# Neighbourhood attention: groups of 112 keys taken as two column halves of 56, side by side in the TensorE array

## The chip, the cores and the metric

The kernel runs on one core of a Trainium2 chip. The metric is the time of one execution on the device in microseconds; the median of several runs counts. The core has TensorE (PE, matmuls; its weight loads are listed apart as PEld), VectorE (DVE), ScalarE (ACT), GpSimd (POOL) and SyncE (SP, which here only issues DMAs). Each engine takes its own instructions in order and waits on semaphores for the others. Matmuls write to PSUM[...]; VectorE and ScalarE read it.

## The reference

The program is two layers of a network on an image x of shape (2, 256, 56, 56): windowed attention, a mixture of experts, a convolution block, and a second mixture of experts. Only the attention is touched. It has 8 heads of 32 channels; each pixel attends to the 7x7 pixels around it:

```python
q = _proj(x, wq, bq).reshape(Bt, NUM_HEADS, hd, Hh, Ww)
k = _proj(x, wk, bk).reshape(Bt, NUM_HEADS, hd, Hh, Ww)
v = _proj(x, wv, bv).reshape(Bt, NUM_HEADS, hd, Hh, Ww)
kw = _windows(k, WINDOW)
vw = _windows(v, WINDOW)
attn = jnp.einsum('bhdxy,bhdxyw->bhxyw', q, kw) * scale
attn = jax.nn.softmax(attn, axis=-1)
out = jnp.einsum('bhxyw,bhdxyw->bhdxy', attn, vw).reshape(Bt, C, Hh, Ww)
```

`_windows` pads by three and stacks the 49 shifted copies; padded positions have key and value zero and count in the softmax.

## The kernel before

The image is cut into 14 strips of 8 rows (7 for each of the two pictures), and a strip into four groups of 14 columns, so that a group has 8x14 = 112 keys. The attention is taken from the side of the keys: the queries that can see any key of a group lie in the 14x20 pixels around it (14 rows by 17 columns in the outer groups of a strip, 11 rows in the strips at the picture's upper and lower edge), that is 280, 238, 220 or 187 queries.

A loop over the strips runs eight steps in each: four groups (`tx`) by two halves of the channels (`c`, four heads each). One step consists of

- `scores`: four f32 matmuls (L1495), one for each head, with 32 rows of keys (32x112) as weights and the queries as moving operand, in four row tiles of the array; then four bf16 matmuls (L1504) that add a mask of -1e30 where a query doesn't see a key, as a product of two small tables (`hot_w`, `far_w`). They go to two PSUM tiles `sc` of two heads (two banks) each, of a pool with two buffers. ScalarE then takes the exponential of each tile (`ex`, L1514).
- `attend`, always of the step before: for each pair of heads `j` two matmuls (L1524) with the values of 112 keys as weights (64 columns: 32 of value and 32 ones, which give the softmax's denominator) into one PSUM bank `av` of a pool with two buffers, and one VectorE addition of that bank into `acc` (L1534), the sums of all queries of the picture in SBUF.
- a piece of `project` for the strip two ahead (layer norm, the transposed `xc`, keys, queries, values), and a piece of what is under way: `leave` (division by the denominators, output projection) and the routing of the first experts.

The program's order is the order on each engine: `scores` of this step, `attend` of the step before, the piece of `project`, the piece of `leave` and routing. All semaphores are set by the framework, from the tiles that an instruction reads and writes. In `project`, queries are evacuated from PSUM by VectorE (L1459), keys by ScalarE (L1455), values by two VectorE additions (L1477), each on a half of one PSUM bank. `blocks` is the view that turns rows of 56 columns into groups of 14; it is used here and in later stages wherever the order of tokens (by groups) meets the order of pixels. Its input `x_tok` is put into token order on the host.

Of the kernel before, what the change touches and what calls it, by code (L numbers as in the profile page):

```python
# [11 lines left out]
F32 = mybir.dt.float32  # L12
# [9 lines left out]
P = 128  # L22
# [20 lines left out]
TT = NQ  # L43
NTT = NT // TT
# [589 lines left out]
def metaformer(ctx: ExitStack, tc: tile.TileContext, a: dict, out: bass.AP, flag):  # L634
# [610 lines left out]
    def blocks(ap):  # L1245

        return ap.rearrange("p h (t w) -> p t h w", w=TW)
# [105 lines left out]
    with ExitStack() as st:  # L1353
# [38 lines left out]
        for n in "vo":  # L1392
            bias[n] = (aw if n == "o" else sw).tile([TT, C], F32, tag=f"b{n}", name=f"b{n}")
            nc.sync.dma_start(bias[n], a[f"L0_conv_b{n}_row"].partition_broadcast(TT))
        hot_w = sw.tile([P, TT], BF16, tag="hot_w", name="hot_w")
        far_w = sw.tile([P, KR, KW], BF16, tag="far_w", name="far_w")
        parts = tp.tile([P, NTT, PAIRS, TT], F32, tag="taken", name="parts", bufs=1)
        far_f = parts[:, 0].rearrange("p j n -> p (j n)")[:, :NK]
        hot_f = parts[:, 1, 0, :]
# [18 lines left out]
        for i in range(3):  # L1418
            t = sw.tile([TT, NTT, PAIRS, 4, HD], F32, tag=f"vals{i}", name=f"vals{i}")
            nc.gpsimd.memset(t[:, :, :, 1:3, :], 1.0)  # L1420
            vals.append(t)
        keys = {}
        norm0, settle0, tiles0, _, gates0, wgt0, counted0, _ = routing(0, aw, tp, ps)

        def project(g):
# [5 lines left out]
            xc = sp.tile([P, KC, NT], F32, tag="xc", name="xc")  # L1431
            for k in range(KC):
# [7 lines left out]
                nc.scalar.copy(xc[:, k, :], px[:, :NT])  # L1440
            yield
            keys[g] = sp.tile([P, KC, NT], F32, tag="keys", name="keys", bufs=3)
            for n in "kq":
                for o in range(KC):
                    pj = ps.tile([P, 512], F32, tag="aux", name="pj")
                    for k in range(KC):
# [3 lines left out]
                            xc[:, k, :],  # L1450
# [7 lines left out]
                    else:  # L1458
                        nc.vector.tensor_scalar_add(  # L1459
                            blocks(q_im[:, o, s * SR : (s + 1) * SR, :]),  # L1460
                            pj[:, :NT].rearrange("p (t h w) -> p t h w", h=SR, w=TW),
                            bias[n][:, o : o + 1],
                        )
                yield
            for t in range(0, NTT, 2):
                pj = ps.tile([TT, 2, C], F32, tag="aux", name="pv")
                for i in range(2):
                    for k in range(KC):
                        nc.tensor.matmul(
                            pj[:, i, :],  # L1470
                            xc[:, k, (t + i) * TT : (t + i + 1) * TT],
# [13 lines left out]
        def scores(g, tx, c):  # L1485

            s = g % NS
            r0, r1 = max(0, s * SR - APAD), min(H, (s + 1) * SR + APAD)
            c0, c1 = max(0, tx * TW - APAD), min(W, (tx + 1) * TW + APAD)
            y0, x0 = APAD - s * SR, APAD - tx * TW  # L1490
            nq = (r1 - r0) * (c1 - c0)
            sc = [sps.tile([TT, 2, 512], F32, tag="sc", name="sc") for _ in range(2)]
            for h in range(4):
                p = slice(HD * h, HD * (h + 1))
                nc.tensor.matmul(  # L1495
                    sc[h // 2][:, h % 2, :nq],
                    keys[g][p, c, tx * TT : (tx + 1) * TT],
                    q_im[p, c, r0:r1, c0:c1],
                    start=True,
                    stop=False,  # L1500
                )
            for h in range(4):
                p = slice(HD * h, HD * (h + 1))
                nc.tensor.matmul(  # L1504
                    sc[h // 2][:, h % 2, :nq],
                    hot_w[p, :],
                    far_w[p, y0 + r0 : y0 + r1, x0 + c0 : x0 + c1],
                    start=False,
                    stop=True,
                )  # L1510
            ex = []
            for j in range(2):
                e = sp.tile([TT, 2, NK], F32, tag="ex", name="ex", bufs=4)
                nc.scalar.activation(e[:, :, :nq], sc[j][:, :, :nq], AF.Exp, scale=HD**-0.5)  # L1514
                ex.append(e)
            return g, tx, c, (r0, r1, c0, c1), ex

        def attend(g, tx, c, window, ex):
            r0, r1, c0, c1 = window
            nq = (r1 - r0) * (c1 - c0)  # L1520
            for j in range(2):
                av = sps.tile([P, 512], F32, tag="av", name="av")
                for i in range(2):
                    nc.tensor.matmul(  # L1524
                        av[VW * i : VW * (i + 1), :nq],
                        vals[g % 3][:, tx, 2 * c + j, 2 * i : 2 * i + 2, :].rearrange(
                            "p a d -> p (a d)"
                        ),
                        ex[j][:, i, :nq],
                        start=True,  # L1530
                        stop=True,
                    )
                d = acc[:, 2 * c + j, r0:r1, c0:c1]
                added = nc.vector.tensor_tensor(  # L1534
                    d, av[:, :nq].rearrange("p (h w) -> p h w", w=c1 - c0), d, ALU.add
                )
            pace[:] = [added.ins]

        def leave(g):
# [36 lines left out]
            for i in range(2):  # L1576
                at = slice(3 * HD * i, 3 * HD * i + HD)
                for j in range(2):
                    to = HD * (2 * j + i)
                    for k in range(KC):  # L1580
                        nc.vector.tensor_tensor(
                            oc[to : to + HD, k, :].rearrange("p (t h w) -> p t h w", h=SR, w=TW),
# [167 lines left out]
    with mid:  # L1750

        with ExitStack() as st:
# [20 lines left out]
            def combine(i):  # L1773
# [13 lines left out]
                for k in range(KC):  # L1787
                    nc.scalar.copy(
                        blocks(inner(*STRIPS[i])[:, :, k]),
                        pu[:, k].rearrange("p (t h w) -> p t h w", h=SR, w=TW),  # L1790
# [296 lines left out]
        with ExitStack() as both:  # L2087
# [17 lines left out]
            def residual(i):  # L2105
# [7 lines left out]
                for at in range(1 + paced):  # L2113
                    for o in range(KC):
# [5 lines left out]
                        if at or not paced:  # L2120
                            nc.scalar.activation(
                                nr[:, o].rearrange("p (t h w) -> p t h w", h=SR, w=TW),
# [158 lines left out]
    with ExitStack() as st:  # L2281
        tp = st.enter_context(tc.tile_pool(name="last_t", bufs=2, reuse_waits="tile"))
        ps = st.enter_context(tc.tile_pool(name="last_ps", bufs=2, space=PSUM, reuse_waits="tile"))
        for i, (b, s) in enumerate(STRIPS):
# [4 lines left out]
            for k in range(KC):  # L2289
                nc.scalar.copy(  # L2290
                    blocks(o[:, k].rearrange("p (h w) -> p h w", w=W)),
                    pu[:, k].rearrange("p (t h w) -> p t h w", h=SR, w=TW),
# [25 lines left out]
def _window_parts():  # L2318


    ky, kx = np.divmod(np.arange(TT), TW)
    rows, cols = np.arange(SR)[:, None], np.arange(TW)[:, None]
    hot = np.concatenate([ky == rows, kx == cols]) * MASKED
    qy, qx = np.divmod(np.arange(NK), KW)
    far = np.concatenate([abs(qy - APAD - rows) > APAD, abs(qx - APAD - cols) > APAD])
# [4 lines left out]
def _laid_out(inputs):  # L2330
    i = {n: np.asarray(v) for n, v in inputs.items()}

    def per_channel(v):
# [5 lines left out]
        i["x"].reshape(B, C, NS, SR, NTT, TW).transpose(0, 2, 3, 5, 4, 1).reshape(-1, TT, NTT, C)  # L2339
# [72 lines left out]
```

## Time and profile before

| | |
|---|---|
| median of three runs | 1844.94 us (1838.95 to 1848.16) |
| profiled execution | 1836.06 us, span of its records 1834.3 us |
| PE, DVE, ACT, POOL busy | 1523.4, 978.8, 701.5, 656.1 us |
| attention loop, first scores to last acc addition | 41.8 to 516 us |
| score matmuls, mask matmuls, attend matmuls | 4 of each in a step, 448 of each |
| acc additions | 224, 0.34 to 0.45 us each |
| exponentials | 224, 0.46 to 0.64 us each |

The page gives for a group of instructions its line, engine, operation and tiles, how many there are, the busy time and mean duration, and the idle time of the engine ahead of it with what ended that. A timeline line gives the start, the duration, the engine, the line, and in brackets the idle time ahead. f32 matmuls are recorded as two instructions each. PEclk is the share of the TensorE clock that was granted.

### The profile page before, as it was taken

The numbers are of one execution on the slowest core, as the hardware profiler recorded it, in microseconds if no ns is written. First come the engines' busy times: TensorE is split into PE (matmuls) and PEld (weight loads), VectorE is DVE, ScalarE is ACT, GpSimd is POOL, SyncE is SP. The second block draws the span as 40 slices with busy tenths as digits, with TensorE's granted clock in tenths as the row PEclk, the third lists the DMA queues.
The fourth block names the chain that finished last, engine by engine and source line by source line (L and its number), as shares of the span: only waits on it lengthen the run. The fifth ranks groups of instructions, "written<-read, shape, count | busy, mean of one in ns | idle before, by whom it ended". The sixth has DMA issues, their size and how long they took to land. (4 is left out here: it accounts for less than half of the span.)

```text
span 1834.3 us, 25840 instructions
## 1 busy us (share of the span) xinstructions
PE 1523.4 (83%) x8612; PEld 1191.8 (65%) x8612; DVE 978.8 (53%) x2690; ACT 701.5 (38%) x1362; POOL 656.1 (36%) x664
## 2 busy tenths in 40 slices
PE   6999998899788858894899799666468799999964
PEld 3555565555466747782788687556457688988953
DVE  4467556476645336855999897675422211111137
ACT  3454433434333324643454443233243333333322
POOL 3012524335343663442244144154553322222210
PEclk9999988999888979996999899755579899999985
DMA  7022324212267757985652000033635568888858
GB/s 241 27 82 83 108 88 122 58 56 83 57 192 232 248 192 265 308 274 161 166 161 61 1 1 1 21 114 99 226 129 186 179 232 273 286 276 294 287 181 311
DMA packets 91886, 291.77 MB, mean 159 GB/s; under 512 B 20487, under 2 KB 35803, under 8 KB 80416
## 3 DMA queue, kind: packets, MB, share of 16 engines
q1 hardware_dynamic: 66736, 231.79, 39.8%
q0 software_dynamic: 21200, 51.82, 8.1%
q10 hardware_dynamic: 3808, 6.42, 1.0%
q8 instruction: 70, 1.15, 0.3%
q14 instruction: 72, 0.59, 0.1%
HBM read 218.51 MB, written 74.20 MB: 160 GB/s over the span
## 5 line engine op out<-in xcount | busy, mean ns | idle before, releaser
L1139 PE MATMUL ph<-ut,w 128*128 128x256 f32 (+1 forms) x1472 | 316.8, 366 | 32.7 <-ACT h L1146 27.5
L1158 PE MATMUL py<-w,h 128*128 128x256 f32 x1288 | 304.1, 385 | 0.0
L1139 PEld LDWEIGHTS ph<-ut,w 128*128 128x128 f32 x1472 | 255.1, 198 | 63.5 <-ACT h L1146 29.0
L1168 DVE TENSOR_TENSOR y<-py,w 128x512 f32<-128x512 f32 (+1 forms) x120 | 76.8, 640 | 409.6 <-PE py L1158 358.2
L888 POOL DMA_INDIRECT xs<-u,pos x224 | 218.1, 974 | 168.6 <-issue 84.4
L1158 PEld LDWEIGHTS py<-w,h 128*128 128x128 f32 x1288 | 247.4, 194 | 34.6 <-DVE y L1168 0.4
L1170 POOL DMA_INDIRECT ys<-y,dest x136 | 136.7, 1005 | 269.9 <-DVE dest L1114 161.0
L1146 ACT ACTIVATE h<-ph,w 128x256 f32<-128x256 f32 (+1 forms) x368 | 162.4, 448 | 115.6 <-PE ph L1139 84.4
L1514 ACT ACTIVATE ex<-sc 112x476 f32<-112x476 f32 (+3 forms) x224 | 117.0, 571 | 207.0 <-PE sc L1504 172.9
L1111 ACT COPY ut<-pt 128x512 f32<-128x512 f32 (+1 forms) x120 | 65.3, 544 | 320.0 <-PE pt L1107 234.2
L1524 PE MATMUL av<-ex,vals 112*64 112x238 f32 (+3 forms) x896 | 125.9, 403 | 16.2 <-DVE acc L1534 15.0
L1534 DVE TENSOR_TENSOR acc<-av,acc 128x238 f32<-128x238 f32 (+3 forms) x224 | 88.1, 408 | 95.4 <-PE av L1524 72.1
L1832 PE MATMUL pc<-lo,wq 128*128 128x448 f32 x336 | 131.5, 393 | 7.3 <-DVE lo L1807 7.2
L1832 PE MATMUL pc<-hi,wq 128*128 128x448 f32 x336 | 131.0, 392 | 3.2 <-DVE x L1856 3.0
L1170 POOL DMA_INDIRECT ys<-y,to x81 | 82.4, 1018 | 128.3 <-DVE dest L1114 74.7
L1975 PE MATMUL pc<-hi,wq 128*128 128x448 f32 (+1 forms) x288 | 102.8, 366 | 18.0 <-ACT hi L1942 9.4
L1229 DVE SCALAR_TENSOR_TENSOR x<-got,wgt,x 112x256 f32<-112x256 f32 x216 | 102.4, 546 | 28.1 <-DMA got<-ys 27.6
L1495 PE MATMUL sc<-q_im,keys 32*112 32x238 f32 (+3 forms) x896 | 95.6, 431 | 11.6 <-ACT ex L1514 7.4
L1975 PE MATMUL pc<-lo,wq 128*128 128x448 f32 (+1 forms) x288 | 101.8, 363 | 0.2 <-DVE lo L1943 0.2
L1524 PEld LDWEIGHTS av<-ex,vals 112*64 112x64 f32 x896 | 57.1, 143 | 66.1 <-issue 26.8
L1107 PE MATMUL pt<-ident,xg 128*128 128x128 f32 x434 | 72.4, 288 | 26.3 <-ACT ut L1111 21.0
L1805 POOL TENSOR_TENSOR v<-pad 128x928 f32<-128x928 f32 (+1 forms) x28 | 56.3, 2023 | 100.3 <-DVE lo L1807 49.1
(273 smaller groups left out, 2467.2 us busy)
## 6 DMA issues: line engine op xcount, KB each, us to landing
w<-in_L_experts SPq DMA_DIRECT2D x64, 1154.0 KB
w<-in_L_experts SPq DMA_DIRECT2D x56, 641.0 KB
xg<-xs SPq DMA_DIRECT2D x97, 260.0 KB
got<-ys SPq DMA_DIRECT2D x28, 896.0 KB
acc<-in_fresh SPq DMA_DIRECT2D x14, 896.0 KB
xt<-in_x_tok SPq DMA_DIRECT2D x14, 448.0 KB
xr<-in_x_tok SPq DMA_DIRECT2D x14, 448.0 KB
rec<-shares SPq DMA_DIRECT2D x28, 224.0 KB
```

The lines of the kernel that those rows point to most:

```text
L888: w = nc.gpsimd.indirect_dma_start(xs[:, :], bass.IndirectOffsetOnAxis(ap=pos[:, j, t0 + t : t0 + t + 1], axis=0), us[t // NTT][:, t % NTT ...
L1139: nc.tensor.matmul(ph[:, :g], w1[:, k, f * P : (f + 1) * P], d["ut"][:, k, :g], start=k == 0, stop=k == KC - 1,)
L1146: nc.scalar.activation(d["h"][:, f, :g], ph[:, :g], AF.Gelu, bias=b1[:, f : f + 1])
L1158: nc.tensor.matmul(py[:, i, :], d["h"][:, f, i * P : (i + 1) * P], w2[:, f, :], start=f == 0, stop=f == NF - 1,)
L1170: o = nc.gpsimd.indirect_dma_start(ys[:, :], bass.IndirectOffsetOnAxis(ap=d["to"][:, i : i + 1], axis=0), y[:, i, :], None, bounds_check=T ...
L1229: nc.vector.scalar_tensor_tensor(xt[:, t, :], y[:, t, j, :], wgt[:, j, n : n + 1], xt[:, t, :], ALU.mult, ALU.add)
L1495: nc.tensor.matmul(sc[h // 2][:, h % 2, :nq], keys[g][p, c, tx * TT : (tx + 1) * TT], q_im[p, c, r0:r1, c0:c1], start=True, stop=False,)
L1514: nc.scalar.activation(e[:, :, :nq], sc[j][:, :, :nq], AF.Exp, scale=HD**-0.5)
L1524: nc.tensor.matmul(av[VW * i : VW * (i + 1), :nq], vals[g % 3][:, tx, 2 * c + j, 2 * i : 2 * i + 2, :].rearrange("p a d -> p (a d)"), ex[j ...
L1534: added = nc.vector.tensor_tensor(d, av[:, :nq].rearrange("p (h w) -> p h w", w=c1 - c0), d, ALU.add)
L1832: nc.tensor.matmul(pc[:, :NT], wq[:, k, c, dx * C + o * P : dx * C + (o + 1) * P], part[:, :, k, dx : dx + W], start=m == 0, stop=m == 2 * ...
L1975: nc.tensor.matmul(pc[:, : 2 * ns * W], wq[:, k, c, dx * C + o * P : dx * C + (o + 1) * P], part[:, : 2 * ns, k, dx : dx + W], start=m == ...
```

## The change

A group of 112 keys becomes two halves of 8 rows by 7 columns, 56 keys each. The queries that see a half lie in 14x13 pixels, 182 (143 in strips of 11 rows); at the picture's side edges the score window is shifted inwards and keeps its 13 columns, and `attend` takes only the 10 columns that see the half. A half takes 64 partitions: the first the partitions 0 to 55, the second 64 to 119.

- `scores`: each head has two matmuls, one for each half, with 56 weight columns, at array columns 0 and 64, and two mask matmuls. `sc` is one tile for the whole loop, four banks, one for each head; the two channel halves `c` share a bank, 256 columns each. It is filled with zeros once, since the exponential now reads all 128 partitions.
- `ex` is taken for two heads at once as before, on 128 partitions and 2x182 elements.
- `attend`: each `j` has four matmuls (two heads by two halves) with 56 rows and 64 columns, and two additions into `acc`, one for each half. `av` is one tile for the whole loop, two banks: one for each half, with both `j` in it, 256 columns each.
- `project`: `xc` holds each half in 64 columns, of which eight stay zero, in two fixed buffers; values are projected with all 128 columns; queries are evacuated by ScalarE.
- Tokens lie by halves; `blocks` works with 7 columns, here and in the later stages, and `x_tok`, `hot` and `far` are laid out to fit.

```diff
+HT = TT // 2
+HW = TW // 2
+HP = P // 2
+WH = HW + WIN - 1
+FAR_W = WH + 2 * APAD
...
-        return ap.rearrange("p h (t w) -> p t h w", w=TW)
+        return ap.rearrange("p h (t w) -> p t h w", w=HW)
...
-            t = sw.tile([TT, NTT, PAIRS, 4, HD], F32, tag=f"vals{i}", name=f"vals{i}")
+            t = sw.tile([P, NTT, PAIRS, 4, HD], F32, tag=f"vals{i}", name=f"vals{i}")
...
+        xcs = []
+        for i in range(2):
+            t = sw.tile([P, KC, 2 * NTT, HP], F32, tag=f"xc{i}", name=f"xc{i}")
+            nc.gpsimd.memset(t[:, :, :, HT:], 0.0)
+            xcs.append(t)
+        sc = sps.tile([P, HEADS // 2, KC, 256], F32, tag="sc", name="sc", bufs=1)
+        av = sps.tile([P, 2, 2, 256], F32, tag="av", name="av", bufs=1)
+        for h in range(HEADS // 2):
+            nc.vector.memset(sc[:, h], 0.0)
...
-                        nc.vector.tensor_scalar_add(
+                        nc.scalar.activation(
                             blocks(q_im[:, o, s * SR : (s + 1) * SR, :]),
-                            pj[:, :NT].rearrange("p (t h w) -> p t h w", h=SR, w=TW),
-                            bias[n][:, o : o + 1],
+                            pj[:, :NT].rearrange("p (t h w) -> p t h w", h=SR, w=HW),
+                            AF.Identity,
+                            bias=bias[n][:, o : o + 1],
                         )
...
-            sc = [sps.tile([TT, 2, 512], F32, tag="sc", name="sc") for _ in range(2)]
+            halves = []
+            for i in range(2):
+                left = (2 * tx + i) * HW
+                c0 = min(max(0, left - APAD), W - WH)
+                halves.append((left, c0, c0 - left + 2 * APAD, slice(HP * i, HP * i + HT)))
             for h in range(4):
                 p = slice(HD * h, HD * (h + 1))
-                nc.tensor.matmul(
-                    sc[h // 2][:, h % 2, :nq],
-                    keys[g][p, c, tx * TT : (tx + 1) * TT],
-                    q_im[p, c, r0:r1, c0:c1],
-                    start=True,
-                    stop=False,
-                )
+                for i, (_, c0, _, at) in enumerate(halves):
+                    nc.tensor.matmul(
+                        sc[at, h, c, :nq],
+                        keys[g][p, c, (2 * tx + i) * HT : (2 * tx + i + 1) * HT],
+                        q_im[p, c, r0:r1, c0 : c0 + WH],
+                        start=True,
+                        stop=False,
+                    )
...
-                e = sp.tile([TT, 2, NK], F32, tag="ex", name="ex", bufs=4)
-                nc.scalar.activation(e[:, :, :nq], sc[j][:, :, :nq], AF.Exp, scale=HD**-0.5)
+                e = sp.tile([P, 2, KR, WH], F32, tag="ex", name="ex", bufs=4)
+                nc.scalar.activation(
+                    e[:, :, : r1 - r0].rearrange("p i h w -> p i (h w)"),
+                    sc[:, 2 * j : 2 * j + 2, c, :nq],
+                    AF.Exp,
+                    scale=HD**-0.5,
+                )
...
+            parts = []
+            for left, c0, _, at in halves:
+                a0, a1 = max(0, left - APAD), min(W, left + HW + APAD)
+                parts.append((a0, a1, slice(a0 - c0, a1 - c0), at, (r1 - r0) * (a1 - a0)))
             for j in range(2):
-                av = sps.tile([P, 512], F32, tag="av", name="av")
                 for i in range(2):
-                    nc.tensor.matmul(
-                        av[VW * i : VW * (i + 1), :nq],
-                        vals[g % 3][:, tx, 2 * c + j, 2 * i : 2 * i + 2, :].rearrange(
-                            "p a d -> p (a d)"
-                        ),
-                        ex[j][:, i, :nq],
-                        start=True,
-                        stop=True,
-                    )
-                d = acc[:, 2 * c + j, r0:r1, c0:c1]
-                added = nc.vector.tensor_tensor(
-                    d, av[:, :nq].rearrange("p (h w) -> p h w", w=c1 - c0), d, ALU.add
-                )
+                    for half, (_, _, cols, at, nq) in enumerate(parts):
+                        nc.tensor.matmul(
+                            av[VW * i : VW * (i + 1), half, j, :nq],
+                            vals[g % 3][at, tx, 2 * c + j, 2 * i : 2 * i + 2, :].rearrange(
+                                "p a d -> p (a d)"
+                            ),
+                            ex[j][at, i, : r1 - r0, cols],
+                            start=True,
+                            stop=True,
+                        )
+                for half, (a0, a1, _, _, nq) in enumerate(parts):
+                    d = acc[:, 2 * c + j, r0:r1, a0:a1]
+                    added = nc.vector.tensor_tensor(
+                        d, av[:, half, j, :nq].rearrange("p (h w) -> p h w", w=a1 - a0), d, ALU.add
+                    )
             pace[:] = [added.ins]
```

## The prediction

> **What bounds the kernel now.** The page comes first. Its chain of waits (part 4) accounts for only a third of the span and names nothing of the attention loop, so it can't be followed back to the change. The place is found from the groups of part 5 and the tiles instead: the score matmuls (tile sc) run from 41.8 to 508.6 us and the acc adds end at 516 us. The loop of 14 strips of 8 steps, 112 steps in all, lasts 474 us. Then busy time by stretch of that loop:
>
> ```profile
> core 0: us, PE busy (x) PEld busy (x) DVE busy (x) ACT busy (x) POOL busy (x), PEclk, DMA share, GB/s
> 42.00:122.00 80.00, 79.97 (x613) 45.38 (x613) 41.75 (x116) 38.95 (x76) 12.73 (x18) 1.00 0.17 55
> 122.00:225.00 103.00, 96.34 (x731) 57.91 (x725) 67.33 (x193) 47.29 (x90) 35.94 (x43) 1.00 0.33 98
> 225.00:351.00 126.00, 114.40 (x766) 70.86 (x764) 71.51 (x208) 45.56 (x92) 46.55 (x54) 0.85 0.31 92
> 351.00:454.00 103.00, 97.43 (x706) 56.73 (x705) 63.94 (x171) 44.82 (x84) 46.33 (x52) 0.98 0.23 67
> 454.00:516.00 62.00, 46.36 (x405) 28.03 (x405) 38.43 (x119) 20.04 (x40) 25.42 (x28) 0.85 0.26 73
> ```
>
> PE is busy for 434.5 of these 474 us (the sum of its column), VectorE for 283, ScalarE for 197. PE sets the pace: whatever lengthens PE's own sequence lengthens the program, and VectorE has room. So the next view is one undisturbed step in order of time:
>
> ```profile
> 149.84 0.68 PE L1495 MATMUL sc<-q_im,keys 32*112 32x238 f32 x8
> 150.34 0.28 PE L1504 MATMUL sc<-far_w,hot_w 32*112 32x238 bf16 x4
> 150.55 1.02 PE L1524 MATMUL av<-ex,vals 112*64 112x238 f32 x8
> 151.22 0.81 DVE L1534 TENSOR_TENSOR acc<-av,acc 128x238 f32<-128x238 f32 x2 [0.52 <-PE av L1524]
> 151.51 1.98 PE L1469 MATMUL pv<-wv,xc 128*112 128x256 f32 x8
> ...
> 153.53 0.76 DVE L1477 TENSOR_TENSOR vals<-pv,bv 112x256 f32<-112x256 f32 x2 [1.50 <-PE pv L1469]
> ```
>
> and the same part of a step with 280 queries:
>
> ```profile
> 436.36 0.75 PE L1495 MATMUL sc<-q_im,keys 32*112 32x280 f32 x8
> 436.94 0.29 PE L1504 MATMUL sc<-far_w,hot_w 32*112 32x280 bf16 x4
> 437.17 1.16 PE L1524 MATMUL av<-ex,vals 112*64 112x280 f32 x8
> 438.26 0.64 PE L1447 MATMUL pj<-xc,wq 128*128 128x448 f32 x1
> ```
>
> From starts to starts, the score phase (sc until av) takes 0.71 us at 238 queries and 0.81 at 280; the attend phase (av until the next group) 0.96 and 1.09. An f32 matmul leaves two records, so x8 is four matmuls. In the score phase all four run beside each other, in attend two and two. The first acc add starts 0.67 us after av; meanwhile PE goes on with the second pair, which has a PSUM tile of its own.
>
> The vals line matters most. PE writes two halves of one bank (i=0, i=1) one after the other, and VectorE adds each half separately. VectorE sat idle for 1.50 us and began the first half only when the matmuls of both were done (151.51 + 1.98 = 153.49). In the trace only the last pv matmul updates a semaphore. So here an engine waits for every access to a bank, also to the half that it doesn't touch.
>
> **What the Trainium skill says.** "PSUM — Partial Sum Buffer", section "PSUM bank collisions raise a hardware error": two engines on one bank and quadrant at once collide, whatever columns they touch, so semaphores have to guard the bank and not the address. The vals wait agrees. "TensorEngine Tiling (Array Packing)", "Key Properties": tiles run in parallel and a change of tiling mode drains the array. The trace agrees on the first: eight records in 0.50 us. The same page, "PSUM Bottleneck": tiling speeds up TensorE and not the evacuation of PSUM. The add rows below agree: they cost by element and by instruction. "TensorE: Matmul & The Clock Gate", "A second HAM failure mode: psum-queue depth-cycling": micro-idles between groups can bring the clock down. The trace has half-clock stretches in this loop (mean clock 0.85 from 225 to 351 us).
>
> **The change, part by part.**
>
> *Score and mask matmuls.* 8 and 8 for 4 and 4 per step, in 32x64 tiles, all eight beside each other, always with 14x13 = 182 queries (143 in strips at the image's edge) for 238 or 280. From 238 to 280 the time from sc to mask grew from 0.50 to 0.58 us, two passes, so 0.95 ns per column and pass; attend grew by 0.13 over four passes, 0.8 ns. I take 0.85. The score phase becomes 0.71 - 2x56x0.85 = 0.62 us: 0.09 or 0.19 less. If the doubled loads show, 0.05 comes back.
>
> *Attend matmuls without waits.* 8 for 4, four beside each other, twice: 0.96 - 4x56x0.85 = 0.77 us, 0.19 or 0.32 less.
>
> *Adds.* Four of at most 182 elements for two of 238 or 280:
>
> ```profile
> L1534 DVE TENSOR_TENSOR acc<-av,acc 128x280 f32<-128x280 f32 x58 | 24.8, 446 | 21.2 <-PE av L1524 14.6 <-remote 3.8 <-PE pj L1447 1.5
> L1534 DVE TENSOR_TENSOR acc<-av,acc 128x238 f32<-128x238 f32 x60 | 23.9, 405 | 30.6 <-PE av L1524 29.1 <-DMA x_mid<-xr 1.1 <-PE sc L1504 0.3
> L1534 DVE TENSOR_TENSOR acc<-av,acc 128x187 f32<-128x187 f32 x24 | 7.8, 351 | 13.4 <-PE av L1524 8.1 <-remote 5.1
> ```
>
> 182 elements cost 0.35 us, so a step costs 1.4 us for 0.81 to 0.89: +0.5 x 112 = 56 us on VectorE. Moving q_im away takes off 28 x 0.67 = 19. VectorE has 320 of 474 us then: no bound by itself.
>
> *The new wait.* Before, av had two buffers and the pairs j=0 and j=1 alternated: an attend waited for adds of the step before. Now av is one tile [P, half, j, 256] of f32: a half's bank holds both j. The matmuls of j=1 follow the adds of j=0 in program order and write the banks that these adds read. By the vals line, PE must wait for both adds. Counted from av's start: adds can begin at 0.67 less two shorter passes (0.10) = 0.57; two adds end at 1.27; 0.05 to release PE (attends that waited for an add here started 0.053 us after its end); then the second half of the attend phase, 0.5 x 0.77 + 0.12 for a refill = 0.50. Attend is 1.82 us for 0.96 or 1.09: +0.86 or +0.73. Below, the wait could cost nothing (if the halves were tracked by columns); above, VectorE's queue is added to it. Behind the waiting matmul stands all of PE's queue: projection, routing, the next scores.
>
> *Net per step*: +0.86 - 0.09 = 0.77 with 238, +0.73 - 0.19 = 0.54 with 280; half of the steps each, 0.65. The 32 steps with 11 rows come to nearly the same, as adds and passes shrink together. 112 x 0.65 = **+73 us**.
>
> *VectorE's queue.* The adds of j=0 stand behind the normalisation (oc, eight of 0.61 us) and residual work, which today's spare av buffer hides. In the strip from 420 to 454 us, replayed by hand with the durations above, PE waits another 0.55, 1.1 and 0.95 us, less 1.59 us that it no longer waits for q_im. Some +1 per strip, up to 3: **+14** (0 to 40).
>
> *What goes away.* Scores wait for exp today (7.4 us on PE, 18.3 on weight loads, not all of it felt); the longer attend covers exp, which shrinks to 128x364 (0.47 us by its rows of 374, 478 ns, and 440, 532 ns): **-10**. PE is idle for 39.5 us of the loop, much of it while ScalarE or POOL finishes a chain of its own; with longer steps some is absorbed: **-12**.
>
> *Clock.* PE idles about 0.45 us more per step, and over 1 us where VectorE is behind. More half-clock windows: **+15** (0 to 45).
>
> *The rest at about nothing.* q_im on ScalarE (28 x 0.63 us, against 27 us saved on exp; ScalarE is 41% busy; uncovered 18). Runs of 7 for 14 in the blocks copies and oc (0 to 7 us on VectorE, 0 to 3 in later stages). Weight loads of 128 for 112 columns in pv hide under 0.22 us passes. Fills of sc, xc and vals at the start lie beside the loads until 41.8 us; uncovered 3. Memory traffic is unchanged.
>
> Sum: 73 + 14 - 10 - 12 + 15 = **+80 us** on the profiled execution's 1836 us, so 1916. The median shown is 1845, 9 us above that execution: **1925**.
>
> **Rivals.** *A, faster:* j=1 isn't held back by the adds of j=0, because the waits go by columns. Then the phases shrink to 0.62 and 0.77: 0.28 or 0.51 less, 0.4 x 112 = 44 us less than 1845, 1801. For it: PE is the bound. Against it: the vals line. It decides where the stall costs less than 0.4 us a step. 7%. *B, about even:* the bank wait exists but most steps cover it, for instance because other waits take the same time today; 1845. Against it: 80 of 80 us busy until 122 us leave nothing to absorb. 5%. *C, much slower:* VectorE's queue and the clock multiply the stall: upper ends 40 and 45 instead of 14 and 15, 1925 + 56 = 1981. For it: the spare buffer that smoothed VectorE's bursts is gone, and the clock already falls to 0.85. 20%. *The forecast:* 68%, 1885 to 1960 on its own.
>
> The range that leaves out A and the extremes of C is 1872 to 1985. Faster by over 0.5% (about what a measurement can tell from no change) 8%, within it 5%, slower 87%.
>
> **What would show it.** The attend group splits in two with an idle of about 0.45 us on PE between, put down to the acc add; step lengths of 2.4 us for 1.67 where no other work lies between; 448 adds near 350 ns; exp no longer waited for; loop end near 595 us. It is wrong if attend runs through in 0.8 us, or if the eight score matmuls take turns.

## The result, and the profile after

The changed kernel takes **1936.97 us** (median of four runs, 1929.5 to 1944.42), the kernel before 1846.55 us beside it: a ratio of 1.0496, with a 95% interval of 1.0439 to 1.0552, so 4.4 to 5.5% slower. The prediction said 1925 us. The profiled execution took 1929.5 us, its records span 1927.7 us: 93 us more than the 1834.3 us of before.

The attention loop, from the first score matmul to the last acc addition, runs from 41.9 to 602.9 us, where it ran from 41.8 to 516.5. That is 561 us for 475, so 86 of the 93 us lie in the loop. The busy time by stretch, as it was shown for the kernel before, with the cuts at the beginnings of strips:

```profile
core 0: us, PE busy (x) PEld busy (x) DVE busy (x) ACT busy (x) POOL busy (x), PEclk, DMA share, GB/s
41.90:132.70 90.80, 82.67 (x1084) 41.17 (x1083) 47.34 (x160) 36.36 (x81) 9.44 (x16) 0.98 0.14 43
132.70:255.20 122.50, 116.20 (x1213) 62.50 (x1213) 70.86 (x233) 46.71 (x99) 38.02 (x41) 0.83 0.27 81
255.20:391.90 136.70, 120.26 (x1245) 67.70 (x1244) 76.12 (x254) 44.27 (x98) 47.37 (x56) 0.81 0.29 87
391.90:515.20 123.30, 109.91 (x1186) 58.69 (x1185) 65.66 (x213) 42.46 (x90) 44.39 (x50) 0.86 0.19 55
515.20:603.00 87.80, 69.46 (x747) 37.24 (x746) 47.16 (x166) 16.32 (x40) 27.20 (x32) 0.61 0.19 52
```

Two things are to be seen. The first row holds strips 0 to 2 (24 steps): PE is idle for 8 of 90.8 us, where it was busy without a gap before, and the three strips take 90.8 us for 79.9, at nearly full clock in both kernels. Below it the clock falls to 0.81 to 0.86, in the last row to 0.61; before, the stretches had 1.00, 1.00, 0.85, 0.98 and 0.85. In this trace the clock is granted either whole or at one half, so each row's time at half clock is 2 x (1 - PEclk) x its length. Over the loop the clock records add up to 198 us at half clock after, and 60 before.

The groups of the page for the same operations as before:

```profile
L1568 DVE TENSOR_TENSOR acc<-av,acc 128x182 f32<-128x182 f32 (+3 forms) x448 | 145.3, 324 | 199.9 <-PE av L1557 151.9
L1539 ACT ACTIVATE ex<-sc 128x364 f32<-128x364 f32 (+1 forms) x224 | 89.8, 451 | 239.7 <-PE sc L1529 187.1
L1557 PE MATMUL av<-ex,vals 56*64 56x182 f32 (+3 forms) x1792 | 139.9, 377 | 40.1 <-DVE acc L1568 36.7
L1519 PE MATMUL sc<-q_im,keys 32*56 32x182 f32 (+1 forms) x1792 | 111.6, 375 | 12.9 <-ACT ex L1539 11.7
```

PE stands idle before attend for 40.1 us, 36.7 of them because of an acc addition (15.0 before); that is only a third of a microsecond per step. The timeline of PE and VectorE in strip 1 shows why it is no more:

```profile
67.46 0.56 PE L1519 MATMUL sc<-q_im,keys 32*56 32x182 f32 x16
...
67.82 0.29 PE L1529 MATMUL sc<-far_w,hot_w 32*56 32x182 bf16 x8
68.04 0.47 PE L1557 MATMUL av<-ex,vals 56*64 56x143 f32 x8
...
68.44 0.70 PE L1452 MATMUL px<-ident,xn 112*128 112x112 f32 x5
68.58 0.61 DVE L1568 TENSOR_TENSOR acc<-av,acc 128x143 f32<-128x143 f32 x2 [0.26 <-PE av L1557]
...
69.15 0.51 PE L1519 MATMUL sc<-q_im,keys 32*56 32x182 f32 x2
69.59 0.47 PE L1557 MATMUL av<-ex,vals 56*64 56x143 f32 x8
69.99 0.40 PE L1519 MATMUL sc<-q_im,keys 32*56 32x182 f32 x7
70.03 0.26 PE L1529 MATMUL sc<-far_w,hot_w 32*56 32x182 bf16 x1
70.13 0.61 DVE L1568 TENSOR_TENSOR acc<-av,acc 128x143 f32<-128x143 f32 x2 [0.93 <-PE av L1557]
```

The attend of a step is in two groups, as predicted: the second begins at 69.59, after the two additions have ended at 69.19. But the time between isn't empty. The compiled program has a piece of the projection (px) and the first score matmul of the next step there, and the rest of those scores after the second group. The section on the kernel before says that the program's order is the order on each engine. For TensorE the compiled program departs from it where there is a wait: in the kernel before, 109 of 112 steps have their attend matmuls in one piece, after, nearly every step has them in two, with other matmuls that the framework's scheduler put between. Here the prediction's picture doesn't fit.

### The profile page after: what moved, and what is told of

The parts are those of the page before. It is cut to its first block, busy times and chain, and to the rows that moved or that the text cites. A ratio compares the mean times of both kernels' runs of the same rounds, so it can differ in the third digit from the quotient of the medians.

```text
span 1927.7 us, 30415 instructions
## 1 busy us (share of the span) xinstructions
PE 1580.1 (82%) x10852; PEld 1196.6 (62%) x10852; DVE 997.9 (52%) x2890; ACT 693.4 (36%) x1390; POOL 656.2 (34%) x666
## 5 line engine op out<-in xcount | busy, mean ns | idle before, releaser
L1568 DVE TENSOR_TENSOR acc<-av,acc 128x182 f32<-128x182 f32 (+3 forms) x448 | 145.3, 324 | 199.9 <-PE av L1557 151.9
L1539 ACT ACTIVATE ex<-sc 128x364 f32<-128x364 f32 (+1 forms) x224 | 89.8, 451 | 239.7 <-PE sc L1529 187.1
L1557 PE MATMUL av<-ex,vals 56*64 56x182 f32 (+3 forms) x1792 | 139.9, 377 | 40.1 <-DVE acc L1568 36.7
L1557 PEld LDWEIGHTS av<-ex,vals 56*64 56x64 f32 x1792 | 53.7, 153 | 126.9 <-DVE acc L1568 76.7
L1519 PE MATMUL sc<-q_im,keys 32*56 32x182 f32 (+1 forms) x1792 | 111.6, 375 | 12.9 <-ACT ex L1539 11.7
L1112 PEld LDWEIGHTS pt<-ident,xg 128*128 128x128 f32 x434 | 56.5, 148 | 57.2 <-issue 29.1
```

Of the source, the lines that this page charges most:

```text
L1112: nc.tensor.transpose(pt[:, k, i * P : (i + 1) * P], d["xg"][:, i, k * P : (k + 1) * P], ident)
L1519: nc.tensor.matmul(sc[at, h, c, :nq], keys[g][p, c, (2 * tx + i) * HT : (2 * tx + i + 1) * HT], q_im[p, c, r0:r1, c0 : c0 + WH], start=Tru ...
L1557: nc.tensor.matmul(av[VW * i : VW * (i + 1), half, j, :nq], vals[g % 3][at, tx, 2 * c + j, 2 * i : 2 * i + 2, :].rearrange("p a d -> p (a ...
L1568: added = nc.vector.tensor_tensor(d, av[:, half, j, :nq].rearrange("p (h w) -> p h w", w=a1 - a0), d, ALU.add)
```

## The experiments

The first theory is the prediction's: with both `j` in one bank (512 f32 values of each partition, the size of the kernel's PSUM tiles of `[P, 512]`), the attend of j=1 waits for the additions of j=0, and the idle time brings the clock down. The main rival is that smaller matmuls and their many changes of tile shape cost the time, wait or no wait.

Chips differ: the kernel before took 1856.29 us on the chip of the first four experiments, 1747.83 on that of the next four, and 1850.46 on that of the last four. So ratios are to the kernel before on the same chip, and loops are compared only where the kernel before took about the same. For each kernel, worked out from the records of its profiled execution: the loop's length, its time at half clock, PE's idle time in it, and how often the tile shape (rows and columns rounded up to 32, 64 or 128) changes from one matmul record to the next. The expectations quoted below took the time at half clock a little too low: 56 us where the records give 60, 194 for 198, 267 for 271.

| kernel | median us | ratio (interval) | loop us | half clock us | PE idle us | changes |
|---|---|---|---|---|---|---|
| before | 1846.55 | 1 | 475 | 60 | 40 | 322 |
| changed | 1936.97 | 1.0496 (1.0439 to 1.0552) | 561 | 198 | 62 | 562 |
| e1_adds_last | 1886.74 | 1.0194 (1.0149 to 1.0238) | 509 | 163 | 84 | 325 |
| e2_merged_adds | 1867.3 | 1.0066 (1.0033 to 1.0099) | 490 | 139 | 79 | 326 |
| e3_before_one_av | 1928.06 | 1.0385 (1.0341 to 1.0428) | 554 | 170 | 24 | 547 |
| e4_q_on_vector | 1953.64 | 1.054 (1.0504 to 1.0575) | 574 | 221 | 68 | 573 |
| e5_before_q_scalar | 1743.13 | 0.9974 (0.9959 to 0.999) | 456 | 47 | 30 | 319 |
| e6_in_order | 1899.35 | 1.0845 (1.0792 to 1.0898) | 611 | 271 | 134 | 310 |
| e7_in_order_filled | 1893.28 | 1.0833 (1.0807 to 1.0859) | 604 | 260 | 129 | 310 |
| e8_merged_q_vector | 1791.36 | 1.0246 (1.0225 to 1.0268) | 498 | 156 | 76 | 336 |
| e9_filled_matmuls | 2016.29 | 1.089 (1.0807 to 1.0972) | 642 | 268 | 110 | 310 |
| e10_in_order_again | 2033.17 | 1.0979 (1.0913 to 1.1045) | 651 | 329 | 161 | 310 |
| e11_merged_again | 1876.44 | 1.0134 (1.0078 to 1.019) | 489 | 140 | 79 | 326 |
| e12_merged_q_vector_again | 1900.23 | 1.0263 (1.0204 to 1.0322) | 519 | 175 | 86 | 336 |

The last three columns show one thing that the first theory doesn't cover. In the eleven kernels with 310 to 340 changes of shape, the time at half clock is 1.5 to 2.5 times PE's idle time. In the three whose groups are cut up (the changed kernel, e3 and e4, with 547 to 573 changes) it is 3.2 to 7.1 times. So idle time as the profile counts it is not all that goes with a low clock here; what else counts isn't shown.

### e1: all attend matmuls ahead of the additions

The changed kernel, with the matmuls of both `j` first and the four additions after them. The work is the same, only the wait inside a step goes.

```diff
             for j in range(2):
                 for i in range(2):
                     for half, (_, _, cols, at, nq) in enumerate(parts):
                         nc.tensor.matmul(
...
+            for j in range(2):
                 for half, (a0, a1, _, _, nq) in enumerate(parts):
```

> The changed kernel, with the matmuls of both j ahead of the four adds in attend, so that the wait inside a step goes and only the wait for the adds of the step before is left. Wait theory (the time lies in the wait of the second attend group for the adds of the first, and in what follows from it: split groups and a falling clock): 1790 to 1850 us, half-clock stretches in the loop well under the 194 us of the changed kernel, near the 56 us of the kernel before. Small-tile theory (the time lies in twice as many small matmuls, weight loads and changes of tile shape): above 1910 us, half-clock time little changed.

Moving the additions takes 52 us off the loop and the changes of tile shape back to 325. The wait inside the step, with the cutting up of groups that goes with it, is the largest part of the loss. It isn't all: the time is above what the first theory expected, and the half-clock time stays at 163 us. The next step's attend still finds both banks taken by the additions just issued: PE's idle time put down to additions is 38.8 us, where the changed kernel has 36.7. PE's idle time in all rises to 84 us; most of the rise (14 us) stands before instructions for which the profile names no wait.

### e2: e1 with one addition for both j of a half

```diff
-            for j in range(2):
-                for half, (a0, a1, _, _, nq) in enumerate(parts):
-                    d = acc[:, 2 * c + j, r0:r1, a0:a1]
-                    added = nc.vector.tensor_tensor(
-                        d, av[:, half, j, :nq].rearrange("p (h w) -> p h w", w=a1 - a0), d, ALU.add
-                    )
+            for half, (a0, a1, _, _, nq) in enumerate(parts):
+                d = acc[:, 2 * c : 2 * c + 2, r0:r1, a0:a1]
+                added = nc.vector.tensor_tensor(
+                    d, av[:, half, :, :nq].rearrange("p j (h w) -> p j h w", w=a1 - a0), d, ALU.add
+                )
```

> As e1_adds_last, with the two j of a half added by one instruction of 2x182 elements: two adds in a step for four. Wait theory: 5 to 20 us below e1_adds_last, since the next step's attend waits for two adds of about 0.54 us instead of four of 0.35. Small-tile theory: as e1_adds_last, above 1910 us.

Another 19 us, down to 0.3 to 1.0% above the kernel before. Its timeline shows the phases without the wait inside the step, and the wait that is left:

```profile
70.80 1.02 DVE L1568 TENSOR_TENSOR acc<-av,acc 128x280 f32<-128x280 f32 x2 [0.96 <-PE av L1557]
...
71.88 0.85 PE L1557 MATMUL av<-ex,vals 56*64 56x182 f32 x16 [0.56 <-DVE acc L1568]
72.66 0.99 PE L1452 MATMUL px<-ident,xn 112*128 112x112 f32 x8
...
73.57 0.56 PE L1519 MATMUL sc<-q_im,keys 32*56 32x182 f32 x16
73.93 0.29 PE L1529 MATMUL sc<-far_w,hot_w 32*56 32x182 bf16 x8
74.14 0.85 PE L1557 MATMUL av<-ex,vals 56*64 56x182 f32 x16
```

The score phase takes 0.57 us (73.57 to 74.14; in the kernel before 0.71 or 0.81) and attend 0.78 us (71.88 to 72.66; before 0.96 or 1.09). So the halves do make PE's own work shorter, by 0.32 us with 238 queries and 0.55 with 280. The single `av` buffer then takes it back: at 71.88 PE has waited 0.56 us for the addition of the step before. At 74.14 it waits for nothing, since a piece of the projection (px) lay between.

### e3: the kernel before with one av buffer

One `av` buffer for two, nothing else: no smaller matmuls, only the wait.

```diff
-                av = sps.tile([P, 512], F32, tag="av", name="av")
+                av = sps.tile([P, 512], F32, tag="av", name="av", bufs=1)
```

> The kernel before, with one buffer for av instead of two: the wait of the second attend group for the add of the first, without the small tiles. Wait theory: 1880 to 1960 us, and more than 120 us at half clock in the loop. Small-tile theory: within 1% of the kernel before, because other work fills the gap.

The kernel before becomes 3.4 to 4.3% slower with its large matmuls. This decides against small matmuls as such, as the origin of a loss of this size. Its timeline shows the same pattern as the changed kernel:

```profile
145.85 0.62 PE L1524 MATMUL av<-ex,vals 112*64 112x238 f32 x4
146.41 0.51 PE L1495 MATMUL sc<-q_im,keys 32*112 32x280 f32 x3
146.43 0.32 PE L1504 MATMUL sc<-far_w,hot_w 32*112 32x280 bf16 x1
146.52 0.41 DVE L1534 TENSOR_TENSOR acc<-av,acc 128x238 f32<-128x238 f32 x1 [1.04 <-PE av L1524]
...
147.47 1.20 PE L1524 MATMUL av<-ex,vals 112*64 112x280 f32 x4
```

Half an attend, then parts of the next scores, then the addition, then the next half (at half clock here). PE's idle time even falls, from 40 to 24 us, while the loop grows by 80. A wait that the scheduler fills shows as more busy time, not as idle time: a group cut in two takes longer than in one piece (two times 0.62 us here for one of 1.02), the scores are cut up as well, and the tile shape changes 547 times for 322. The first two strips show this price alone, since they have no half clock and hardly any idle time. First the kernel before:

```profile
41.80:65.10 23.30, 23.27 (x195) 13.69 (x195) 10.83 (x30) 11.31 (x24) 6.73 (x8) 1.00 0.28 89
65.10:91.30 26.20, 26.20 (x204) 14.31 (x203) 11.24 (x31) 12.85 (x24) 1.43 (x3) 1.00 0.06 19
```

and then e3:

```profile
42.40:69.20 26.80, 26.63 (x193) 13.16 (x192) 11.13 (x30) 11.27 (x24) 6.46 (x8) 1.00 0.22 73
69.20:99.00 29.80, 29.62 (x201) 13.41 (x200) 11.39 (x31) 12.72 (x24) 1.42 (x3) 1.00 0.05 16
```

That is 7.1 us in 16 steps, 0.44 us per step. How it divides between longer groups and changes of shape wasn't tried. Over the whole loop e3 is also 170 us at half clock for 60, with less idle time than before.

### e4, e5, e8, e11 and e12: who takes q_im

e4 is the changed kernel with q_im back on VectorE; e5 is the kernel before with q_im on ScalarE; e8 and e12 are e2 with q_im on VectorE, and e11 is e2 again beside e12.

```diff
-                        nc.scalar.activation(
+                        nc.vector.tensor_scalar_add(
                             blocks(q_im[:, o, s * SR : (s + 1) * SR, :]),
                             pj[:, :NT].rearrange("p (t h w) -> p t h w", h=SR, w=HW),
-                            AF.Identity,
-                            bias=bias[n][:, o : o + 1],
+                            bias[n][:, o : o + 1],
                         )
```

> The changed kernel with the queries evacuated by VectorE again (28 instructions of about 0.67 us). Wait theory: 0 to 15 us above the changed kernel, as the adds stand behind them in VectorE's queue. A theory in which ScalarE's new work holds up the exponentials: 5 us or more below the changed kernel.

> The kernel before, with only the evacuation of the queries moved from VectorE to ScalarE. If VectorE's queue is what delays the attend matmuls and the output projection there (PE waits for q_im 8 us, for acc adds 15 us): 5 to 20 us below the kernel before. If ScalarE's queue then holds up the exponentials: 0 to 15 us above it.

> e2_merged_adds with the queries evacuated by VectorE again. If ScalarE's queue holds up the exponentials in e2_merged_adds (PE waits 19 us for them, weight loads 30): 3 to 15 us below e2_merged_adds. If VectorE's queue counts, as between the changed kernel and e4_q_on_vector: 3 to 15 us above it.

> All attend matmuls ahead of the adds and one add for both j of a half, q_im on ScalarE, once more, as what e12 is compared with on the same chip. Every theory: 1.003 to 1.010 times the kernel before.

> As e11, with q_im's addition back on VectorE. If VectorE's queue sets when the one PSUM buffer of a step comes free (first theory), it is 8 to 35 us above e11, as the loop's 498 us against 490 and the ratios of two different chips suggest. If the difference between these ratios came from the chips alone (rival), it is within 6 us of e11.

In the kernel before, the move to ScalarE is worth 4.7 us (0.1 to 0.4%): e5 is the one version that beats both kernels, by little. In e2's arrangement it is worth more: 24 us between e12 and e11 on one chip, where the 28 additions of q_im come to 19 us of VectorE. (e8 came out 1.8% above e2 by the ratios, some 30 us where 3 to 15 were expected, but on another chip; hence e11 and e12.) Between e4 and the changed kernel it is about 8 us by the ratios, which is within their intervals. e11 itself came out at 1.3%, above what was expected of it, though its interval overlaps that of e2. So VectorE's queue does reach PE, but not where the expectation put it. PE's idle time before attend for acc additions is the same in both, 37.6 us in e11 and 36.8 in e12; what e12 has instead is 13.2 us of waiting for q_im itself, as the kernel before has 8.0, and 35 us more at half clock. That the missing spare buffer makes the difference isn't shown.

### e6 and e10: the program's order

The changed kernel, with scores, the pieces of the projection and attend each held behind the one before, so that nothing moves into the gap.

```diff
+        def behind(at):
+            return tc.issue_after(at[-1]) if at else nullcontext()
...
-                    here = scores(g, tx, c)
+                    with behind(attended):
+                        here = scores(g, tx, c)
...
-                        attend(*before)
+                        with behind(scored):
+                            attend(*before)
```

> The changed kernel with TensorE's order as the program writes it: both attend groups directly behind each other, no other group moved between them. Wait theory as the prediction has it (a stall of about 0.45 us on PE in each step; other groups in the gap are a help): 10 to 50 us above the changed kernel, PE idle in the loop over 100 us for 62. Rival, that the splitting of groups and the 562 changes of tile shape in the loop (322 before) cost more than the stall: 5 to 30 us below the changed kernel.

> The kernel in the program's order once more, as what e9 is compared with on the same chip. Both theories: 1.08 to 1.09 times the kernel before.

This is the kernel that the prediction described, and its step looks as described:

```profile
75.70 0.47 PE L1563 MATMUL av<-ex,vals 56*64 56x143 f32 x8
...
76.24 0.61 DVE L1574 TENSOR_TENSOR acc<-av,acc 128x143 f32<-128x143 f32 x2 [0.26 <-PE av L1563]
76.91 0.47 PE L1563 MATMUL av<-ex,vals 56*64 56x143 f32 x8 [0.74 <-DVE acc L1574]
77.31 0.56 PE L1524 MATMUL sc<-q_im,keys 32*56 32x182 f32 x16
```

The additions begin 0.54 us after attend, the second half follows 1.21 us after the first, some 0.05 us after the additions' end at 76.85, and attend in all takes 1.61 us with 143 queries. But this kernel is 8 to 10% above the kernel before, not 4%: PE is idle for 134 and 161 us, and half clock takes 271 and 329 us. By the ratios e6 is some 64 us above the changed kernel, more than the 50 expected at most. The rival of tile shapes, wait or no wait, falls once more: with the fewest changes of all (310) it is the slowest. The rescheduling that the prediction overlooked saves about half of the loss.

### e7 and e9: filling the gap

e7 puts eight weight loads of 64x64 between the two attend groups of e6, e9 eight bf16 matmuls into a PSUM tile that nobody reads. Both are meant to keep TensorE busy while it would stand idle, and do nothing else. The edit of e9:

```diff
+                if j == 0:
+                    spare = ps.tile([P, 512], F32, tag="aux", name="spare")
+                    idle = far_w[:HP].rearrange("p h w -> p (h w)")
+                    for n in range(8):
+                        side = HP * (n % 2)
+                        nc.tensor.matmul(
+                            spare[side : side + HP, : KR * FAR_W],
+                            all_w[:HP, :HP],
+                            idle,
+                            start=True,
+                            stop=True,
+                        )
```

> As e6_in_order, with eight idle weight loads of 64x64 between the two attend groups, where PE waits anyway. Clock theory (PE's idle gaps bring the clock down, and half-clock time makes up a good part of the loss): if weight loads count as activity, half-clock time in the loop falls by 40 us or more against e6_in_order and the time by 10 to 40 us. If the clock has little to do with it, or if weight loads don't count: within 10 us of e6_in_order, half-clock time the same.

> The kernel in the program's order, with eight matmuls of 64x64 weights and 266 columns, of which nobody reads the result, put on TensorE between the two groups of attend matmuls of a step, that is into the stall of about 0.85 us. If the low clock follows from TensorE's idle time (first theory), idle time of TensorE in the attention loop falls from 134 us to 40 to 80, the time at half clock falls from 267 us below 200, and the time is 15 to 50 us below that of the same kernel without them (e10), although TensorE does more. If the low clock has another cause, or its price is small (rival), the time at half clock stays within 30 us of e10's and the time is the same as e10's or longer by what the matmuls don't fit into the stall, 0 to 60 us.

e7 tells nothing: its loads are over in about 0.2 us, in part beside the attend matmuls, and leave PE's idle time where it was (129 us for 134). e9's matmuls do fill the gap:

```profile
71.75 0.47 PE L1563 MATMUL av<-ex,vals 56*64 56x143 f32 x8
...
72.05 0.63 PE L1577 MATMUL spare<-far_w,all_w 64*64 64x266 bf16 x8
72.29 0.61 DVE L1586 TENSOR_TENSOR acc<-av,acc 128x143 f32<-128x143 f32 x2 [0.17 <-PE av L1563]
...
72.96 0.47 PE L1563 MATMUL av<-ex,vals 56*64 56x143 f32 x8 [0.29 <-DVE acc L1586]
```

With more for TensorE to do, the kernel is 17 us below e10 (2016.29 for 2033.17), and the mean clock of its four executions is higher (0.832 to 0.837 for 0.821 to 0.826). The cleanest part is the first five strips, strip by strip. First e9:

```profile
41.90:75.30 33.40, 27.66 (x404) 16.15 (x403) 12.26 (x47) 11.04 (x26) 5.17 (x7) 0.90 0.15 46
75.30:108.20 32.90, 27.37 (x429) 16.32 (x428) 13.90 (x45) 12.11 (x26) 1.42 (x3) 1.00 0.05 16
108.20:145.10 36.90, 30.87 (x441) 19.16 (x440) 22.17 (x68) 14.19 (x30) 5.18 (x7) 1.00 0.20 57
145.10:186.90 41.80, 37.97 (x465) 23.83 (x464) 22.54 (x69) 15.26 (x32) 7.55 (x8) 0.88 0.23 69
186.90:234.10 47.20, 41.33 (x477) 26.09 (x476) 27.16 (x87) 15.26 (x32) 7.91 (x10) 0.82 0.24 74
```

and then e10, without the matmuls:

```profile
41.60:74.30 32.70, 26.33 (x345) 14.30 (x344) 12.32 (x47) 11.13 (x26) 5.18 (x7) 0.79 0.14 45
74.30:110.00 35.70, 28.75 (x364) 14.77 (x364) 14.01 (x45) 12.21 (x26) 1.42 (x3) 0.81 0.05 14
110.00:153.10 43.10, 35.14 (x381) 19.16 (x380) 22.17 (x68) 14.29 (x30) 5.18 (x7) 0.76 0.19 56
153.10:196.10 43.00, 35.19 (x401) 20.77 (x400) 22.59 (x69) 15.26 (x32) 7.53 (x8) 0.84 0.20 60
196.10:242.60 46.50, 34.70 (x414) 20.84 (x414) 27.06 (x87) 15.26 (x32) 7.91 (x10) 0.87 0.25 77
```

VectorE, ScalarE and POOL do the same work to about 0.1 us a strip; TensorE has the matmuls put in, and PEclk differs. The time at half clock is 74 us in e10 and 34 in e9, and the five strips take 201.0 and 192.2 us. So in this pair TensorE's gaps do bring the clock down, and 40 us less at half clock saved 8.8 us: **0.22 us for each us at half clock**. That is a low estimate. In e9 the pauses between the two groups are 3.7 us longer over these strips in all (2.2, 1.8 and 1.1 us longer in one step of each of the first three, where VectorE has its normalisation, t_stats, ahead of the additions or among them, and 1.6 us shorter in the fifth); strip 0 even takes longer than in e10, with half as much at half clock. Without these 3.7 us the price would be 0.31, and a fit over strips 0 to 12 of the ten kernels before e9, with a constant for each kernel and each strip, gives 0.38. So the price is an estimate of 0.2 to 0.4. Idle time in the loop is 110 us for e10's 161, where 40 to 80 were expected, and that the half-clock time would fall below 200 us was too much: in the later strips some gaps grow over 2 us, longer than eight matmuls fill. "TensorE: Matmul & The Clock Gate" of the Trainium skill, section "A second HAM failure mode: psum-queue depth-cycling", has idle times between groups bringing the clock down; this pair agrees. Which length of gap tips the clock wasn't tried.

## Why the prediction was right, and where not

**Right: the time, and the wait.** 1925 us against 1936.97, within the range. The step that decided it, that the attend of j=1 waits for the additions of j=0 although they read other columns of the bank, is shown by the changed kernel's timeline, by e6, by e1, which takes 52 us off the loop by moving the additions alone, and by e3, which puts the wait alone into the kernel before and costs 3.85%. Rivals A and B (1801 and 1845) fall. That the wait goes by the bank isn't shown: a group of matmuls carries one wait here. In the timeline of e6 the addition from the first half's bank ended at 76.55 us by its single record, but the first matmul of j=1, which writes that bank alone, began at 76.91, 0.05 us after the addition from the other bank. The vals line of the prediction can't tell either, as there the bank is also a tile.

**Right: the phases and the additions.** Score phase 0.62 us predicted, 0.57 measured; attend without waits 0.77 predicted, 0.78 measured; additions near 350 ns for 182 elements, measured 346 on average; exp at 0.47 us, measured 0.468. All eight score matmuls of a step lie beside each other. The loop's end was put near 595 us and is at 602.9.

**Wrong picture: PE's order.** The prediction had "behind the waiting matmul stands all of PE's queue: projection, routing, the next scores", and from that 0.45 us idle per step. The scheduler takes just these and puts them into the gap. PE's idle time in the loop grew by 23 us, not by 50 (0.45 x 112), and the loss shows as busy time: two groups of 8 records with 182 queries take 2 x 0.54 = 1.08 us where 16 together take 0.85, the next scores are cut into pieces, and tile shapes change 562 times for 322.

**Wrong: what goes away.** The prediction took off 10 us because the scores would no longer wait for the exponentials. They wait longer: 11.7 us on PE for 7.4, and 24.1 us on the weight loads for 18.3. In the kernel before, each pair of heads had its own `sc` tile, and in 30 of 111 steps the scores began before the second exponential of the step before had ended. In the changed kernel, with one `sc` tile for all four heads, no step does. That the single tile is the cause is likely, but no run has two. The 12 us of PE's idle time that longer steps would absorb didn't show either, as idle time grew.

**Two parts of the sum mis-sized, in opposite directions.** The direct terms were +73 (net per step), +14 (VectorE's queue), -10 and -12 (what goes away): 65 us, or 0.58 per step. In strips 0 to 2, where the clock was nearly full in both kernels, 24 steps grew by 10.9 us, of which some 1 is clock: 0.41 per step (0.31 in the first two strips, 0.6 in the third), or 46 us in 112 if the other strips are like them. The *clock* term was +15 and was far too small: 138 us more at half clock, at 0.22 to 0.38 each, are an estimate of 30 to 52 us, at or above the upper end of its range of 0 to 45. That leaves 34 to 56 of the 86 us for the direct terms. So the sum came out by luck: too much in the direct terms, too little in the clock. e1 agrees from the other side: without the wait inside the step the loop is 52 us shorter, with 35 us less at half clock (8 to 13 us), so some 40 us for the wait itself.

**Program order would have been worse than predicted.** For the kernel that the text described, e10, strips 0 to 2 take 111.5 us for 79.9. Less their 48 us at half clock at 0.22 to 0.38, that is 13 to 21 us in 24 steps, 0.6 to 0.9 per step where 0.58 was predicted. The larger part is the clock: 269 us more at half clock than before are, at the same price, 59 to 102 us, where the prediction had 15. Over the program it is +9.8%, not +4.3%. By the ratios of e6 and e10, the change in program order would be 156 to 181 us slower than the 1846.55 us of before, where the prediction's sum had 80.

**VectorE's queue** matters: e12 against e11 shows 24 us for 19 us of work moved onto VectorE, though without more waiting for the additions, by which the prediction reasoned. The term's own size in the changed kernel (+14) wasn't measured apart.

**Open:** why e2 isn't faster than the kernel before, with phases shorter by 0.32 to 0.55 us per step. Its phases save 0.4 x 112 = 45 us, yet its loop is 15 us longer, so some 60 us have to be found. PE's idle time is 40 us larger, 26 of them before attend for additions of the step before (41.2 us for 15.0), and 79 us more at half clock are an estimate of 17 to 30 us. That is about the size; whether a second pair of `av` banks would bring the gain out wasn't tried.

## What to carry to other kernels

A PSUM tile that takes the place of two alternating ones can turn every eviction (the read that empties it) into a wait: count the buffers, not the matmuls, and put all matmuls of a tile ahead of the evictions that read it, as e1 did for 52 us. Don't assume that a wait stays where the text has it: look for what a scheduler can move into it, and look for its price in busy time and cut-up groups as much as in idle time. Where a change makes TensorE stop often, or cuts up its groups, price the clock as a term of its own: here the extra half-clock time was larger than the extra idle time by six.

## What was not expected of the hardware

- The clock costs less than its name says: a us at half clock cost an estimated 0.2 to 0.4 us in this loop, though single groups take much longer then (attend of half a step 0.89 for 0.54 us). Part of such a stretch is spent waiting for other engines; that this is the whole reason isn't shown.
- A low clock doesn't need idle time that the profile shows: e3 has less of it than the kernel before (24 us for 40) and almost three times as much time at half clock (170 us for 60).
- In e10 VectorE and ScalarE at times stand still with their input ready; the profile names no engine of this core ("remote"), 31 us before the additions of the loop and none in e6, the same program on another chip:

```profile
292.42 0.53 PE L1563 MATMUL av<-ex,vals 56*64 56x182 f32 x8
293.26 0.94 POOL L893 DMA_INDIRECT xs<-u,pos  x1 [0.30 <-issue]
...
295.02 0.71 ACT L1545 ACTIVATE ex<-sc 128x286 f32<-128x286 f32 x2 [5.78 <-remote]
296.46 0.69 DVE L1574 TENSOR_TENSOR acc<-av,acc 128x182 f32<-128x182 f32 x2 [3.68 <-remote]
```

The attend group ended at 292.95, the addition that reads it began at 296.46. POOL issues gathers of rows meanwhile; whether they are the cause wasn't tried. This is why e9 and e10 are compared on their first five strips, which have none of it.
